# A four-layer graph network on one core: preparation that starts with the layer norm, and one visit per gathered block

## The chip, the cores and the metric

The kernel runs on one core of a Trainium2 chip. The metric is device time in microseconds (us). Engine names are those of the profile: PE is the matrix engine (PEld its weight loads), DVE the vector engine, ACT the scalar engine, POOL the engine that issues the indirect DMAs here, SP the engine that issues most plain DMAs. A name with a q behind it (SPq, POOLq) is that engine's instruction queue.

## What is computed

There are 6250 nodes with 256 features and 100000 edges (src, dst), the edges sorted by dst. The input is layer-normed and cut at zero, then four times each node adds the sum of its in-neighbours and goes through a three-matrix perceptron; the result is added to the input.

```python
def agg(h):
    return jax.ops.segment_sum(h[src], dst, num_segments=N)
for l in range(NL - 1):
    h = x + agg(x)
    h = jax.nn.relu(h @ W1s[l] + b1s[l])
    h = jax.nn.relu(h @ W2s[l] + b2s[l])
    x = h @ W3s[l] + b3s[l]
h = x + agg(x)
h = jax.nn.relu(h @ cW1 + cb1)      # cW1 256x256
h = jax.nn.relu(h @ cW2 + cb2)      # cW2 256x64
return h @ cW3 + cb3                # cW3 64x256
# around it: h = relu(layernorm(x)); x = x + network(h)
```

## The kernel before

The nodes are 49 blocks of 128. `XY` holds, in SBUF, all blocks of the current layer, already multiplied by that layer's W1 (the last W3 and the next W1 are multiplied together ahead, `fused`), as a high part and a rest so that two fast fp32r products give an fp32 one. The layers are called l0 to l3 here. Sums over neighbours are made in two ways.

*Products.* For about half of the blocks, a matrix of edge counts (uint8) is built once, in l0, out of one-hot rows of the edges (`build`: one-hots `lo` and `hi` on DVE at L1035, their product on PE at L1076, two copies per step to the matrix by ACT at L1084 and by DVE at L1086, in turn). It is kept in DRAM (`mats`), fetched again in each later layer in chunks of seven blocks (`fetch`), cast to fp32r (`prepare`, L1565) and multiplied with XY on PE: L1588 block by block in l0, L1665 by panels of four blocks after it (`product`). A unit of a panel is one block of XY: four matmuls with 512 columns. These matmuls are called `agg` below, by the tile that they write.

*Gathers.* For the other blocks (23 in l0, 20 in l1, 20 in l2, 19 in l3, 82 in all) the rows of the neighbours are fetched from the layer's table in DRAM: 17 tiles of 128 rows per block, each by one indirect DMA that POOL issues (L1382, 1394 in all, called rows below), and summed on PE by products with one-hots (`hot`, made by DVE at L1402) in a visit (`add`, L1419). `ROUNDS` gives two visits per block, of 11 and 12 matmuls over 8 and 9 tiles.

The order of the work is fixed while the program is written. `tick` counts units of the products, `passed` adds the estimated PE time of each product to a clock, and `Gathered.flow` issues a gather each time that clock has moved by a pace that spreads a layer's gathers over the layer. `meets` says when a visit is due: when the clock has reached the time of its last gather (the first one `LEAD` = 21 us after `begin`), or 8 units ahead of the layer's end. `begin(l+1)` comes when every block of the table of layer l+1 is written: after the perceptron of the last gathered block (block 48) and of the last panel. Those blocks' perceptrons are written out in three steps (transposes at L1479; L1225/L1233, L1245 and L1287/L1290) among the next layer's first products. In the page a line that carries PE `ps` is of these steps.

Ahead of the products stands the preparation. `look` finds, from the edge list, where each half block's edges start and what the lists of rows are: a first gather of the edges near each start (`near_i`), 17 counts over them (11 on DVE at L695, 6 on ACT at L698), an index chain, and then some 45 gathers of edge windows by POOL, called by `ask`. `normed` loads the input (`xs`), makes the statistics (`moments`, L879/L880), scales (L899), transposes, multiplies with W1 (L908, L920) and writes XY (L932 to L940), for 25 pairs of blocks. `fused` multiplies W3 and W1. All three are generators that the loop at the start of the kernel turns by `next`: it runs `look` and `fused` to the end of the index chain first, and then the 25 pairs with the rest of `look` between them.

Of the kernel before, what the change touches and what calls it, by code (L numbers as in the profile page):

```python
# [17 lines left out]
P = 128  # L18
# [378 lines left out]
def sorted_edges(  # L397
# [59 lines left out]
    ROUNDS = ((3, 1, -1), (0, 4, 2))  # L457
# [3 lines left out]
    NEAR = 11 * P  # L461
# [36 lines left out]
    rel = const.tile([P, left[NQ] // T, len(ROUNDS), 3, P // Q], BF16, name="rel")  # L498
# [58 lines left out]
    def fused(pool, w3_aps, w1_aps):  # L557
# [9 lines left out]
        load(1)  # L567
        yield
        for l in range(NLAYER):
            w3, w1 = loaded[l]  # L570
            w3t = pool.tile([P, KC, C], F32, name="w3t", bufs=1)
# [6 lines left out]
            b3b = pool.tile([P, KC, P], F32, name="b3b", bufs=1)  # L578
            nc.gpsimd.tensor_copy(b3b, b3[l][:, :, None].to_broadcast([P, KC, P]))
            yield  # L580
            w = pool.tile([P, KC + 1, C], F32, name="w31", bufs=1)
            for i in range(KC + 1):
                ps = ps_m.tile([P, W], F32, name="ps")
                for k in range(KC):
                    left = w3t[:, k, i * P:(i + 1) * P] if i < KC else b3b[:, k, :]
# [4 lines left out]
            load(l + 2)  # L590
# [26 lines left out]
    def look(pool):  # L617
        firsts_i = pool.tile([1, EB], I32, name="near_i", bufs=1)
        with nc.allow_non_contiguous_dma(reason="each tile's first destination"):
# [6 lines left out]
        nc.sync.dma_start(out=run[:FULL, :], in_=bass.AP(tensor=dst.tensor, offset=dst.offset,  # L626
                                                         ap=[[EC, FULL], [1, EC + 1]]))
        nc.sync.dma_start(out=run[FULL:FULL + 1, :E - FULL * EC],
                          in_=dst[FULL * EC:E].rearrange("(o e) -> o e", o=1))
# [15 lines left out]


        half = pool.tile([P, 2], F32, name="half", bufs=1)
        junk = pool.tile([P, NEAR], BF16, name="junk", bufs=1)
        for h in range(2):
# [3 lines left out]
                             start=True, stop=True)  # L653
            nc.vector.tensor_scalar(junk[:NSUB, e0:e1], ps[:NSUB, :e1 - e0], low[:NSUB, 0:1], None,
# [11 lines left out]
        )  # L666
        yield
# [24 lines left out]
        DV = 11  # L692
        for q in range(GSUB + 1):
            if q < DV:
                nc.vector.tensor_scalar(junk[:NSUB], near[:NSUB], float(GD * q), None,  # L695
                                        op0=OP.is_lt, op1=OP.add, accum_out=less[:NSUB, q:q + 1])
# [4 lines left out]
        nc.vector.tensor_scalar(less[:NSUB, DV:], less[:NSUB, DV:], -0.5, float(NEAR // 2),  # L701
                                op0=OP.mult, op1=OP.add)
        first = pool.tile([P, GSUB + 1], F32, name="first", bufs=1)
        nc.vector.tensor_scalar(first[:NSUB], less[:NSUB], at[:NSUB, 0:1], None, op0=OP.add)
        starts = pool.tile([NSUB, GSUB], I32, name="starts", bufs=1)
        nc.vector.tensor_scalar(starts, first[:NSUB, :GSUB], float(E - P), None, op0=OP.min)
        wd = pool.tile([P, GSUB, P], I32, name="wd", bufs=1)
        ws = pool.tile([P, GSUB, P], I32, name="ws", bufs=1)
        for q in range(GSUB):
            for w, e in ((wd, dst), (ws, src)):  # L710
                asks.append((w[:NSUB, q, :], e, starts[:, q:q + 1]))
        ask(4)
# [4 lines left out]
        sel = pool.tile([P, NQ, PW], F32, name="near_i", bufs=1)  # L717
# [17 lines left out]
        nc.vector.tensor_tensor(sel[:NSUB], sel[:NSUB], some[:NSUB], OP.mult)  # L735
        ps = ps_m.tile([P, W], F32, name="ps")
        for q in range(NQ):
            nc.tensor.matmul(ps[:PW, NV * q:NV * q + NV], sel[:NSUB, q, :], both[:NSUB, :],
                             start=True, stop=True)
        spread = pool.tile([P, NQ, NV], F32, name="spread", bufs=1)  # L740
# [77 lines left out]
        for w, (q0, q1) in ((3, (0, NQ - 1)), (4, (NQ - 1, NQ))):  # L818
            rows = gone[q0][1] * T
            nc.vector.tensor_reduce(wrong[:rows, w:w + 1], off[:rows, q0:q1, :],  # L820
                                    axis=mybir.AxisListType.XY, op=OP.max)
        ask(len(asks))
# [8 lines left out]
        yield  # L831
# [957 lines left out]
```

## Time and profile before

| | us |
|---|---|
| median of 3 runs | 2129.72 (2128.97 to 2136.23) |
| the profiled execution | 2135.8, its span 2134.0 |
| preparation: start to the last write of XY | 124.7 |
| first build steps, up to the first product | 124.7 to 142.7 |
| gathers of l0 / l1 / l2 / l3, issue of the first to the last | 126.6–674.2 / 719.2–1163.3 / 1205.7–1647.6 / 1686.8–2105.0 |
| last gather to the end of the span | 29.0 |

The profile puts 2057.4 us of the span on PE as busy time (96%), 1445.4 us on POOL (68%), 937.7 on DVE and 864.3 on ACT. The row of PE's waits has 15.0 us on gathered rows, in 12 waits. In the timeline rows of the trace, a row is a run of like instructions: start, busy time, engine, line, operation, tiles, count, and in brackets the idle time ahead of it with what ended it. A visit of 11 or 12 matmuls shows as 22 or 24 PE records, since an fp32 matmul leaves two. In the window rows, each engine's busy time stands with its count of instructions in brackets, then the clock that PE was granted, the DMA share and GB/s.

### The profile page before, as it was taken

To read this page: it belongs to the slowest core of one execution; us is meant where nothing else is said; L and a number is where in the kernel's file an instruction comes from. 1 tells how busy PE (TensorE), PEld (TensorE's weight loads), DVE (VectorE), ACT (ScalarE), POOL (GpSimd) and SP (SyncE) were. 2 spreads that over 40 slices of the span, in tenths; PEclk is the share of its full clock that TensorE was granted. 3 is DMA by queue.
4 is the path that set the end of the run, shared out by engine and by line. 5 is a ranking of instruction groups with operands and counts; after the bars stand their busy time and mean duration, and the time that the engine had idled before them with its cause. 6 is when DMAs were issued, how large, how long until landed. Compare 5 with 4: busy or idle time off the path is not lost.

```text
span 2134.0 us, 33393 instructions
## 1 busy us (share of the span) xinstructions
PE 2057.4 (96%) x12076; PEld 1487.8 (70%) x12076; DVE 937.7 (44%) x2192; ACT 864.3 (41%) x1775; POOL 1445.4 (68%) x1470
## 2 busy tenths in 40 slices
PE   4979999999999999999999999999999999999997
PEld 3756766667667777777776777777776777777675
DVE  7877867667673422222233322222233433333332
ACT  4856655556556522323232433222333432223231
POOL 2727777777774477777776377777776277777773
PEclk9979999999999999999999999999999999999999
DMA  5524545545455655455455554555456555556553
GB/s 157 176 98 139 162 142 153 158 140 164 150 158 152 213 163 155 153 181 164 142 186 167 173 160 148 173 165 169 146 168 195 170 172 181 184 180 194 183 160 119
DMA packets 184901, 347.61 MB, mean 163 GB/s; under 512 B 32446, under 2 KB 118496, under 8 KB 184726
## 3 DMA queue, kind: packets, MB, share of 16 engines
q0 software_dynamic: 68960, 185.41, 29.7%
q1 hardware_dynamic: 113838, 158.12, 22.3%
q8 instruction: 97, 1.59, 0.3%
q10 hardware_dynamic: 1928, 1.85, 0.3%
q14 instruction: 78, 0.64, 0.1%
HBM read 287.98 MB, written 57.26 MB: 162 GB/s over the span
## 4 chain that ended last, share of the span: by engine, by line
PE 88%; DVE 5%; DMA 4%; issue 1%; ACT 1%; POOL 1%; SPq 0%; DVEq 0%; POOLq 0%; ACTq 0%
PE agg L1665 43%; PE agg L1588 16%; PE sums L1419 11%; PE ps L1233 6%; PE ps L1290 6%; PE bp L1076 4%; DMA rows<-table,idx 3%; PE ps L1479 1%; POOL rows L1382 1%; DVE junk L695 1%; PE bp L920 1%; DVE hi L1035 1%; DVE at L1086 1%; PE ps L1245 0%; DMA table<-zs 0%
## 5 line engine op out<-in xcount | busy, mean ns | idle before, releaser
L1382 POOL DMA_INDIRECT rows<-table,idx x1394 | 1387.7, 995 | 611.4 <-issue 220.6
L1665 PE MATMUL agg<-a,XY 128*128 128x512 f32 x4116 | 982.8, 395 | 1.9 <-DVE clT L1600 1.9
L1665 PEld LDWEIGHTS agg<-a,XY 128*128 128x128 f32 x4116 | 764.6, 188 | 209.5 <-issue 45.8
L1565 ACT CAST a<-at 128x512 fp32r<-128x512 uint8 (+1 forms) x542 | 326.9, 616 | 576.9 <-PE agg L1665 543.9
L1565 DVE CAST a<-at 128x512 fp32r<-128x512 uint8 x543 | 242.7, 448 | 552.8 <-PE agg L1665 469.3
L1588 PE MATMUL agg<-XY,a 128*128 128x512 f32 x1470 | 404.9, 409 | 1.3 <-DVE un L1600 0.7
L1588 PEld LDWEIGHTS agg<-XY,a 128*128 128x128 f32 x1470 | 258.9, 189 | 53.7 <-issue 8.7
L1419 PE MATMUL sums<-rows,hot 128*32 128x256 f32 x3772 | 256.0, 385 | 16.2 <-DMA rows<-table,idx 15.0
L1419 PEld LDWEIGHTS sums<-rows,hot 128*32 128x32 f32 x3772 | 112.6, 109 | 142.6 <-issue 53.6
L1549 ACT CAST a<-at 128x512 fp32r<-128x512 uint8 (+2 forms) x362 | 196.7, 574 | 6.5 <-PE agg L1588 6.5
L1084 ACT CAST at<-bp 128x392 uint8<-128x392 f32 x240 | 116.6, 487 | 203.7 <-PE bp L1076 191.0
L1086 DVE CAST at<-bp 128x392 uint8<-128x392 f32 x240 | 135.1, 563 | 138.2 <-PE bp L1076 138.2
L1448 DVE TENSOR_TENSOR u<-u,sums 128x256 f32<-128x256 f32 x82 | 34.3, 419 | 241.8 <-PE agg L1665 226.9
L1076 PE MATMUL bp<-hi,lo 128*128 128x196 bf16 x960 | 127.5, 255 | 11.0 <-DVE hi L1035 10.7
L1290 PE MATMUL ps<-w,h 128*128 128x256 f32 x588 | 133.9, 379 | 1.4 <-ACT h L1236 0.9
L1233 PE MATMUL ps<-h,w 128*128 128x512 f32 (+3 forms) x332 | 133.9, 545 | 0.6 <-DVE zz L1298 0.6
L1035 DVE TENSOR_TENSOR hi<-cols,pairs 128x784 bf16<-128x784 bf16 x240 | 134.3, 560 | 0.0
L1076 PEld LDWEIGHTS <-lo 128*128 128x128 bf16 x960 | 70.6, 99 | 81.9 <-DVE hi L1035 27.8
L1290 PEld LDWEIGHTS ps<-w,h 128*128 128x128 f32 x588 | 111.1, 190 | 18.7 <-ACT h L1236 1.8
L1483 ACT ACTIVATE h<-ps,bias 128x256 f32<-128x256 f32 (+1 forms) x116 | 47.2, 464 | 154.9 <-PE ps L1479 154.9
L1298 DVE TENSOR_TENSOR zz<-ps,w 128x512 f32<-128x512 f32 (+1 forms) x75 | 50.1, 678 | 117.0 <-PE ps L1290 117.0
L1035 DVE TENSOR_TENSOR lo<-lanes,pairs 128x512 bf16<-128x512 bf16 x240 | 100.3, 418 | 1.3 <-ACT pairs L1030 1.3
(171 smaller groups left out, 989.7 us busy)
## 6 DMA issues: line engine op xcount, KB each, us to landing
at<-mat SPq DMA_DIRECT2D x151, 448.0 KB
mat<-at SPq DMA_DIRECT2D x30, 784.0 KB
rows<-table,idx POOLq DMA_INDIRECT x1394
table<-zz SPq DMA_DIRECT2D x72, 256.0 KB
back<-table SPq DMA_DIRECT2D x99, 128.0 KB
xs<-in_x_dram SPq DMA_DIRECT2D x8, 768.0 KB
table<-zs SPq DMA_DIRECT2D x24, 256.0 KB
out_dram<-zz SPq DMA_DIRECT2D x24, 256.0 KB
```

The costliest lines, as they stand in the source:

```text
L1035: nc.vector.tensor_tensor(o.rearrange("p q (n t) -> p q n t", t=2), values.rearrange("p (n t) -> p n t", t=2)[:, None, :, :].to_broadcast( ...
L1076: mm = nc.tensor.matmul(bp[:, m * HW:(m + 1) * HW], lo[:, q + m, :], hi[:, q + m, :], start=True, stop=True)
L1084: nc.scalar.copy(o, v)
L1086: nc.vector.tensor_copy(o, v)
L1233: mm = nc.tensor.matmul(ps[:mp, :w], weights[l][0][:, c, i * P:i * P + mp], h1[:, c, :w], start=(c == 0), stop=(c == KC - 1))
L1290: mm = nc.tensor.matmul(o, h2[0][:, c, nodes], w3[:, c, :], start=(c == 0), stop=(c == KC - 1))
L1382: got = nc.gpsimd.indirect_dma_start(out=t, out_offset=None, in_=tables[self.l][:, :], in_offset=bass.IndirectOffsetOnAxis(ap=idx[:, o:o + ...
L1419: nc.tensor.matmul(self.sums[m * Q:(m + 1) * Q, :C], self.hot[:, (c - min(rounds)) // 2, m, :], self.rows[g, c + 4 * m], start=(c == ROUND ...
L1549: nc.scalar.copy(a[:, i * m * P:(i + 1) * m * P].rearrange("p (j d) -> p j d", j=m), counts[b][:, j:j + m, :])
L1565: cast(o, at[:, :, d:d + m * P])
L1588: mm = nc.tensor.matmul(agg, a[:, d:d + P], XY[:, j, :], start=(j == 0), stop=(j == NT - 1))
L1665: mm = nc.tensor.matmul(agg[c][:, :w], XY[:, j, o:o + P], a[:, :w], start=(j == 0 and half == 0), stop=(j == NT - 1 and half == 1))
```

## The change

1. *Preparation.* The loop over the pairs starts at once, and `look` is turned by one stage at each of its steps (28 stages, 30 steps), `fused` by one in the first nine. The counts (`less`) are spread one or two to a step: 8 on DVE and 9 on ACT, over 1280 edges in place of 1408; the windows of four starts are asked for as soon as their counts stand (`settled`), three gathers per step in the first nine steps, then two. The moments of the first pair stand ahead of `look`'s second stage; the moments run 4 pairs ahead in place of 6. Stages end where DVE would need the result of PE (`yield` behind matmuls). The two loads of `run` stand behind the first two loads of xs; W3 and W1 of the second layer are loaded one stage later; the copy `b3b` on POOL is gone.
2. *Build.* The first 24 copies of the build are all on ACT.
3. *Visits.* `ROUNDS` has one visit per block, of 23 matmuls over 17 tiles. Its one-hots are made 4 units after the visit before; `hot` is one buffer of 768 columns in place of two of 384. The lead becomes `MARGIN` = 6 us and one visit's 17 gathers.
4. *The layers' ends.* In l1 and l2 the last visit may stand behind the layer's own products, up to 10 units into the next layer (`LATE`, `TAIL`; l0 and l3 keep the values of before). `open_one` keeps the old layer's visits first. Products take the seven chunks of XY in the order 0, 1, 3, 4, 5, 6, 2.
5. *Buffers.* 27 gather tiles in place of 25, 8 casts in place of 9 in l1 to l3.

DVE in the preparation, where the counts stand. Before (`junk,less` is a count, L891/L892 end a group of moments):

```order
L891 RECIPROCAL rstd<-std 128x6
L892 SCALAR_TENSOR_TENSOR shift<-mv,rstd 128x6
L689 TENSOR_SCALAR near<-near_i,low 98x1408
L695 TENSOR_SCALAR junk,less<-near 98x1408 x11
L701 TENSOR_SCALAR less<-less 98x6
L704 TENSOR_SCALAR first<-less,at_f 98x17
L706 TENSOR_SCALAR starts<-first 98x16
L720 TENSOR_SCALAR both<-first,since 98x1
```

The same place in the change, a few steps on:

```order
L904 RECIPROCAL rstd<-std 128x6
L905 SCALAR_TENSOR_TENSOR shift<-mv,rstd 128x6
L699 TENSOR_SCALAR less<-less 98x2
L701 TENSOR_SCALAR first<-less,at_f 98x4
L705 TENSOR_SCALAR starts<-first 98x4
L713 TENSOR_SCALAR junk,less<-near 98x1280
L945 COPY zs<-bp 128x512
L892 BN_STATS stats<-xs 128x6
L893 BN_AGGR mv<-stats 128x2
```

The eleven counts in a row are now single ones, with the pairs' moments and copies (`zs`) between them.

PE where l1 passes into l2. Before, the last visits of l1 (both halves of block 48's, `sums`) stand 32 `agg` matmuls ahead of the end of l1's products:

```order
L1665 MATMUL agg<-a,XY 128x512 x16
L1479 MATMUL ps<-ident,u 128x128 x2
L1479 MATMUL ps<-ident,clT 128x128 x2
L1419 MATMUL sums<-rows,hot 32x256 x23
L1665 MATMUL agg<-a,XY 128x512 x8
L1479 MATMUL ps<-ident,u 128x128 x2
L1665 MATMUL agg<-a,XY 128x512 x4
```

In the change the visit of block 48 stands 36 `agg` matmuls behind that end:

```order
L1700 MATMUL agg<-a,XY 128x512 x20
L1506 MATMUL ps<-ident,u 128x128 x2
L1506 MATMUL ps<-ident,clT 128x128 x2
L1700 MATMUL agg<-a,XY 128x512 x8
L1446 MATMUL sums<-rows,hot 32x256 x23
L1700 MATMUL agg<-a,XY 128x512 x8
L1506 MATMUL ps<-ident,u 128x128 x2
L1256 MATMUL ps<-h_12329,w_8629 128x512 x4
```

The visit, and behind it the perceptron of block 48 and so the start of l2's gathers, moved by 68 `agg` matmuls.

PE at the end of l3, from the last visit on. Before:

```order
L1419 MATMUL sums<-rows,hot 32x256 x12
L1665 MATMUL agg<-a,XY 128x512 x8
L1479 MATMUL ps<-ident,u 128x128 x2
L1665 MATMUL agg<-a,XY 128x512 x8
L1245 MATMUL ps<-clT,h_20696 128x256 x4
L1665 MATMUL agg<-a,XY 128x512 x12
L1233 MATMUL ps<-h_20730,w_16886 64x128 x2
L1665 MATMUL agg<-a,XY 128x512 x8
L1287 MATMUL ps<-clT,h_20786 128x256
```

In the change:

```order
L1446 MATMUL sums<-rows,hot 32x256 x23
L1700 MATMUL agg<-a,XY 128x512 x8
L1506 MATMUL ps<-ident,u 128x128 x2
L1700 MATMUL agg<-a,XY 128x512 x4
L1248 MATMUL ps<-h_20413,w_16837 64x256 x4
L1700 MATMUL agg<-a,XY 128x512 x12
L1268 MATMUL ps<-clT,h_20534 128x256 x4
L1700 MATMUL agg<-a,XY 128x512 x12
L1256 MATMUL ps<-h_20522,w_16837 64x128 x2
L1700 MATMUL agg<-a,XY 128x512 x8
L1310 MATMUL ps<-clT,h_20595 128x256
L1700 MATMUL agg<-a,XY 128x512 x20
```

Behind both stand the last panel's own two steps. 64 `agg` matmuls follow the last visit, where 36 did.

Counted over the whole order of PE from the first product on (a group is a run of matmuls of one kind, the build's left out; block 48's last step is what `begin` of the next layer stands behind):

| place on PE | groups, before | after | `agg` matmuls, before | after |
|---|---|---|---|---|
| last visit of l1 | 463 | 422 | 2663 | 2731 |
| last step ahead of `begin` of l2's gathers | 477 | 431 | 2723 | 2771 |
| last visit of l2 | 591 | 519 | 4080 | 4120 |
| last step ahead of `begin` of l3's gathers | 604 | 531 | 4136 | 4168 |
| last visit of l3 | 717 | 622 | 5550 | 5522 |
| the end | 732 | 640 | 5586 | 5586 |

The core of the diff:

```diff
-    ROUNDS = ((3, 1, -1), (0, 4, 2))
+    ROUNDS = ((3, 1, -1, 0, 4, 2),)
-    NEAR = 11 * P
+    NEAR = 10 * P
...
-        DV = 11
-        for q in range(GSUB + 1):
-            if q < DV:
-                nc.vector.tensor_scalar(junk[:NSUB], near[:NSUB], float(GD * q), None,
-                                        op0=OP.is_lt, op1=OP.add, accum_out=less[:NSUB, q:q + 1])
-            else:
-                nc.scalar.activation(junk2[:NSUB], near[:NSUB], AF.Sign, bias=edge[:NSUB, q:q + 1],
-                                     accum_out=less[:NSUB, q:q + 1])
-                yield
...
+        for q in range(0, GSUB, 2):
+            nc.vector.tensor_scalar(junk[:NSUB], near[:NSUB], float(GD * q), None,
+                                    op0=OP.is_lt, op1=OP.add, accum_out=less[:NSUB, q:q + 1])
+            for k in (q + 1,) if q + 2 < GSUB else (q + 1, q + 2):
+                nc.scalar.activation(junk2[:NSUB], near[:NSUB], AF.Sign, bias=edge[:NSUB, k:k + 1],
+                                     accum_out=less[:NSUB, k:k + 1])
+            yield
+            if q % 4 == 2:
+                settled(q - 2, q + 2)
+        settled(GSUB, GSUB + 1)
...
-        for t0 in range(0, 4 * G, G):
+        for t0 in (0, G):
             load(t0)
         yield
-        for s in range(G):
+        moments(0)
+        yield
+        for t0 in (2 * G, 3 * G):
+            load(t0)
+        for s in range(1, LEAD):
             moments(s)
...
+            next(looked)
+            next(rows)
             next(looked)
...
+            next(rows)
             next(looked)
-            next(rows)
-            turn_biases()
-            for _ in range(2 * NLAYER):
-                next(looked)
-                next(ahead_w)
-            next(looked)
-            STAGES = (*range(4, 20, 2), 20, 22, 24)
+            STAGES = (*range(16), 17, *range(17, 28))
             for i, _ in enumerate(rows):
-                ask(2)
+                ask(3 if i < 9 else 2)
+                if i == 1:
+                    turn_biases()
+                if i < 2 * NLAYER + 1:
+                    next(ahead_w, None)
                 if i in STAGES:
                     next(looked, None)
...
-                    if step % 2:
+                    if step % 2 or step <= 2 * PRE:
                         nc.scalar.copy(o, v)
...
-                return now[0] >= ends[self.l] - 8 or clock[0] >= self.first + (
+                return now[0] >= ends[self.l] + LATE[self.l] or clock[0] >= self.first + (
                     self.upto[self.done + 1] - self.upto[1]) * self.pace
             def begin(self):
-                self.first = clock[0] + LEAD
-                self.end = begun[self.l] + work_of(self.l) - TAIL
-                self.pace = (self.end - self.first) / (self.upto[-1] - self.upto[1])
+                self.one_hots(0)
+                self.end = begun[self.l] + work_of(self.l) - TAIL[self.l]
+                self.pace = (self.end - clock[0] - MARGIN) / self.upto[-1]
+                self.lead = MARGIN + self.upto[1] * self.pace
+                self.first = clock[0] + self.lead
...
                 if self.done < self.n:
-                    self.one_hots(self.done)
+                    later(4, lambda v=self.done: self.one_hots(v))
...
-        LEAD, TAIL = 21.0, 10.0
+        MARGIN = 6.0
+        TAIL = [10.0] + [-5.0] * (NLAYER - 1) + [10.0]
+        LATE = [-8] + [10] * (NLAYER - 1) + [-8]
...
-            for j in range(NT):
+            for at, j in enumerate(c * CH + i for c in CHUNKS for i in range(CH)):
...
-        rings = ctx.enter_context(tc.tile_pool(name="rings2", bufs=AHEAD + 6))
+        rings = ctx.enter_context(tc.tile_pool(name="rings2", bufs=AHEAD + 5))
-        gath = ctx.enter_context(tc.tile_pool(name="gath2", bufs=25))
+        gath = ctx.enter_context(tc.tile_pool(name="gath2", bufs=27))
```

More of the change, by code (lines that the diff above doesn't have):

```diff
@@ L971, in sorted_edges @@
             next(rows)
+            ahead_w = fused(prep, [W3s[l] for l in range(NLAYER)],
+                            [W1s[l + 1] for l in range(NLAYER - 1)] + [cW1])
+            next(ahead_w)
             make_identity(nc, ident)
@@ L1158, in sorted_edges, with split @@
         BACK = 3
-        def split(j, m, z):
+        fresh = set()
+        def split(l, j, m, z):
+            fresh.update((l + 1, k) for k in range(j, j + m))
             nc.scalar.copy(XY[:, j:j + m, :C], z[:, :m, :])
@@ L1661, in product @@
                 a = ring.pop(u)
+                assert (l, j) in fresh, (l, j, now[0], ends[l - 1], [k for k in range(NT) if (l, k) not in fresh], len(queue), layers[l - 1].done)
                 for c in range(KC):
```

114 lines of the change are left out of this document (66 added, 48 removed).

## The prediction

> **What bounds the kernel now.** I read the page first, for the engine that is busy throughout and for the one whose instructions never get shorter.
>
> ```profile
> span 2134.0 us, 33393 instructions
> PE 2057.4 (96%) x12076; PEld 1487.8 (70%) x12076; DVE 937.7 (44%) x2192; ACT 864.3 (41%) x1775; POOL 1445.4 (68%) x1470
> L1382 POOL DMA_INDIRECT rows<-table,idx x1394 | 1387.7, 995 | 611.4 <-issue 220.6
> ```
>
> PE looks like the bound at 96%. But POOL's gathers take 995 ns each, and 220.6 us more went by ahead of them in "issue", that is, in nothing that the profile shows. So a row costs POOL clearly more than its busy time, and 68% can be full. The windows by layer show where: from the first gather of a layer to the last one, and the gaps between.
>
> ```profile
> 719.00:1163.00 444.00, 442.57 (x2517) 324.02 (x2515) 132.61 (x305) 140.76 (x258) 336.67 (x339) 1.00 0.56 173
> 1163.00:1205.00 42.00, 37.64 (x155) 27.05 (x156) 13.34 (x31) 14.60 (x32) 0.99 (x2) 0.92 0.28 85
> 1205.00:1648.00 443.00, 443.00 (x2520) 325.00 (x2518) 132.31 (x297) 138.86 (x251) 333.72 (x340) 1.00 0.56 173
> 1648.00:1687.00 39.00, 35.69 (x163) 26.05 (x163) 14.79 (x34) 15.57 (x34) 0.78 (x2) 1.00 0.31 95
> 1687.00:2105.00 418.00, 411.98 (x2452) 303.16 (x2452) 135.31 (x299) 125.39 (x226) 319.88 (x322) 1.00 0.58 183
> 2105.00:2134.00 29.00, 18.41 (x98) 10.87 (x94) 8.22 (x19) 3.13 (x7) 0.95 (x1) 0.85 0.24 81
> ```
>
> Columns are PE, PEld, DVE, ACT, POOL. In l1 and l2 PE has work in practically every microsecond, and POOL issues 340 rows in 443 us, 1.30 each. In l3 POOL issues 322 in 418, also 1.30 each, while PE idles for 6 us. The same 1.30 with PE full and with PE waiting: I take it as POOL's own rate. So l1 and l2 end when PE is done, with POOL close behind, and l3 ends when POOL is done. The gaps of 42 and 39 us are those in which the next table is not complete.
>
> ```profile
> PE sums L1419 <- DMA rows<-table,idx: 15.0, 12, 3.3
> 1159.03 1.92 PE L1419 MATMUL sums<-rows,hot 128*32 128x256 f32 x26
> 1161.35 0.62 PE L1419 MATMUL sums<-rows,hot 128*32 128x256 f32 x2 [0.40 <-DMA rows<-table,idx]
> 1163.55 0.64 PE L1419 MATMUL sums<-rows,hot 128*32 128x256 f32 x8 [1.58 <-DMA rows<-table,idx]
> 1167.38 1.92 PE L1419 MATMUL sums<-rows,hot 128*32 128x256 f32 x10 [3.19 <-DMA rows<-table,idx]
> 1169.22 3.78 PE L1665 MATMUL agg<-a,XY 128*128 128x512 f32 x8
> 1172.81 0.56 PE L1479 MATMUL ps<-ident,u 128*128 128x128 f32 x2
> 1652.49 1.05 PE L1419 MATMUL sums<-rows,hot 128*32 128x256 f32 x10 [3.28 <-DMA rows<-table,idx]
> ```
>
> Of PE's 15.0 us of waits on rows, 5.2 (.40+1.58+3.19) stand at l1's last visits and 3.3 at l2's.
>
> **The price of a group on PE.** Every visit breaks a run of `agg` matmuls.
>
> ```profile
> 1127.18 1.50 PE L1419 MATMUL sums<-rows,hot 128*32 128x256 f32 x24
> 1128.61 3.94 PE L1665 MATMUL agg<-a,XY 128*128 128x512 f32 x16
> 1132.38 3.60 PE L1233 MATMUL ps<-h,w 128*128 128x512 f32 x8
> 2086.57 8.48 PE L1665 MATMUL agg<-a,XY 128*128 128x512 f32 x36
> 2094.89 0.60 PE L1479 MATMUL ps<-ident,u 128*128 128x128 f32 x4
> ```
>
> Start to start, 16 `agg` take 3.77 us and 36 take 8.32, so one is .2275 and .13 is left for the change of group. A visit of 12 is 1.43, so .108 each, and a visit of 23 is 2.49 + .13.
>
> **Up to l3's first gather.** By the table of counts, 73 groups fewer stand ahead of it (604 to 531): −9.5. But 32 more `agg` do (4136 to 4168), since block 48's step moved into the next layer: +7.3. Net −2.2. The 5.2 and 3.3 of waits have some 68 and 40 matmuls of cover more, 15 and 9 us, and go. With them goes the slow stretch behind the first: 1167.38 to 1169.22 is 1.84 for five matmuls worth .67, and the eight `agg` take 3.59 where 1.95 is right, 2.8 together. These three are −11.3. What is late next: l0's last visit wants 17 rows where its second half wanted 9 and is not moved, for which I put +2 (between 0 and the 3.3 of the longest wait). In l2 PE's own work from `begin` to the last visit is 1349 `agg` (307), 20 visits and 88 groups (59), and the perceptrons' matmuls, some 81 from their rows: 447, against 340 rows at 1.30 and 4 of landing, 446. That is level, where l1 keeps 18 us; +2 for it, between 0 and 5. So, counted from the first product, l3's first gather comes 2.2 + 11.3 − 2 − 2 = 9.5 earlier; the ends are 13.5 (neither of the two late ones) and 5.2 (3.3 and 5 of them).
>
> **l3 and the end.** The 323 gathers take 418 as before. PE's own work to the last visit sinks from some 409 to 390 (1354 `agg`, 19 visits, 91 groups, 26 of perceptrons), so POOL has more than 30 us of room to be waited for, and nothing that PE saves here counts. Behind the last visit there are 64 `agg` in place of 36, +6.4, and three more groups, +.4. So from the first product on: −9.5 + 6.8 = −2.7, with ends −6.7 and +1.6. POOL takes most of what PE gives.
>
> **Preparation.** Here the windows show DVE.
>
> ```profile
> 9.30:125.00 115.70, 88.85 (x416) 68.48 (x414) 96.40 (x270) 74.71 (x160) 54.99 (x64) 0.93 0.49 152
> 48.40:91.00 42.60, 40.60 (x211) 32.30 (x210) 40.86 (x117) 35.15 (x77) 33.27 (x33) 0.98 0.60 178
> 91.00:125.00 34.00, 28.91 (x132) 22.65 (x130) 23.25 (x67) 20.29 (x47) 12.88 (x11) 0.85 0.38 118
> 22.80 0.94 DVE L689 TENSOR_SCALAR near<-near_i,low 98x1408 f32<-98x1408 int32 x1
> 23.77 1.62 DVE L695 TENSOR_SCALAR_CACHE_REDUCE junk<-near 98x1408 bf16<-98x1408 f32 x1
> 25.44 1.62 DVE L695 TENSOR_SCALAR_CACHE_REDUCE junk<-near 98x1408 bf16<-98x1408 f32 x1
> 41.95 0.17 DVE L701 TENSOR_SCALAR less<-less 98x6 f32<-98x6 f32 x1
> 48.38 0.42 DVE L879 BATCH_NORM_STATS2 stats<-xs 128x6 f32<-128x256 f32 x1
> 123.72 1.02 DVE L940 TENSOR_TENSOR XY<-zs,XY 128x512 fp32r<-128x512 f32 x2
> ```
>
> DVE is 96% busy up to 91 and 68% after it, where the pairs wait in the chain through PE. The counts go from 11 at 1.67 (23.77 to 25.44) to 8 at 1.52 (10/11): −6.2 of DVE; ACT, at 74.7 of 115.7, takes three more. Two ways to the new end agree. By busy time: 96.4 − 6.2 = 90.2, at 96% 94.0, from 9.3 on: 103; and the 10.8 idle of 91 to 125, which is the drain of the chain: 114. By steps: the 30 steps from 48.38 to 124.7 took 2.5 each with `look`'s rest in them; the new ones carry also its chain (41.95 to 48.38, 6.4) and eight counts (12.2), +.62: 30 × 3.1 from 22 on is 116. I take 115, −10; ends are 103 (−21) and 124.7 (0). The gathers of windows start at four counts instead of all, and at POOL's rate they fill some 60 us, so they hide. `run`, the later loads and POOL's missing copy: nothing, as first readers come steps later; cover gone, a load waits under 2.
>
> **First build steps.**
>
> ```profile
> 126.89 0.42 DVE L1035 TENSOR_TENSOR lo<-lanes,pairs 128x512 bf16<-128x512 bf16 x1
> 127.23 0.56 DVE L1035 TENSOR_TENSOR hi<-cols,pairs 128x784 bf16<-128x784 bf16 x1
> 127.71 0.56 DVE L1086 CAST at<-bp 128x392 uint8<-128x392 f32 x1
> 128.18 0.42 DVE L1035 TENSOR_TENSOR lo<-lanes,pairs 128x512 bf16<-128x512 bf16 x1
> 125.00:142.00 17.00, 5.69 (x12) 0.61 0.45 151
> 131.70 0.83 PE L1076 MATMUL bp<-hi,lo 128*128 128x196 bf16 x4 [0.45 <-DVE hi L1035]
> ```
>
> DVE does a double step in 1.29 (126.89 to 128.18), .47 of it the copy; PE waits for DVE. Twelve copies go to ACT, which then has two of .47 (5.69 for 12, the window row of L1084) per double step, .95. So ACT sets the step: 12 × (1.29 − .95) = −4; ends −5.7 (DVE alone) and 0.
>
> **Sum.** −10 − 4 − 2.7 = −16.7, on the execution's 2135.8: 2119. The median lies 6.1 lower, at 2129.72: 2113. All the good ends give −21 − 5.7 − 6.7 = −33, 2096; the bad ones 0 + 0 + 1.6, 2131. Hot's single buffer, the casts' ring and the chunk order: nothing, DVE is at 44% and the visits' one-hots stand 4 units, some 4 us, after the last use; the two more gather tiles are POOL's and I see no idle of POOL for want of one.
>
> **The clock.** After 5.2 us of waits PE worked at half rate from 1167.38 on, 2.8 us lost (above). In l3 the change makes 32 us of waits in 19 visits, 1.7 each, some of them twice that. The Trainium skill ("TensorE: Matmul & The Clock Gate", Part 1) says that one idle window of about 3.4 us sets the half rate; the trace agrees, with the .92 of clock in the window 1163 to 1205 beside 1.00 in the window that follows. By that rule single waits of 1.7 would do nothing and the sum stays; where waits come in a row between late rows, it is the last rival below.
>
> **Rivals.**
> - *The pairs don't come earlier.* For: `look`'s stages stand in each step, and ACT, with 9 counts, the scales and the W copies, sits in the pairs' chain. Against: DVE's 96%, so it had been DVE. Then −6.7: 2123.
> - *Slower: a step of the preparation waits.* A stage of `look` that needs POOL or PE holds DVE, and now the pairs with it. At 4.5 per step the preparation ends at 22 + 135 = 157: +32 − 6.7, 2155. It decides from 4.0 per step on (142: +17.3 − 6.7, which is .5%). For: nine steps have a count each on DVE (1.52) and ACT, a W stage on PE and three gathers, 3.9 us at 1.30; against: 2.5 per step so far, while ACT and PE had room.
> - *PE is the bound throughout.* All 92 groups (−12), all 15.0 of waits, the slow stretch (−2.8) and −14 of the start: 2086. It needs l3's gathers at 390/323, 1.21 each; no layer shows that.
> - *Half clock in l3.* If half of the 19 waits set it off at 2.8 each, those intervals are 23.3 in place of 22: 9.5 × 1.3 = +12, 2125. It limits itself, as a slowed PE no longer waits.
>
> **How the numbers follow.** My forecast 0.49, the pairs no earlier 0.23, slower 0.16, PE the bound 0.06, half clock 0.06. About 0.5%, 10.6 us, is what a measurement tells from no change, so the bounds are 2119 and 2140. Faster: most of the forecast (.43), PE the bound (.06), and a part of the first rival (.05): 0.54. Slower: 0.16. Same: the rest, 0.30. The range 2098 to 2138 leaves out PE the bound and the slower case past 2138, some 0.2.
>
> **What would show it.** The last write of XY near 115; the double build steps near .95, bound by ACT's copies; no row wait at l1's and l2's ends, but several in l3, one per visit; rows in l3 at 1.30 without a gap; from the last gather to the end some 35 in place of 29. It is wrong if steps of the preparation take 3.5 or more, or if l2's last visit waits long, as POOL's 446 there has no room.

## The result, and the profile after

| | before | after |
|---|---|---|
| median, us (20 runs each) | 2132.12 (2127.09 to 2138.86) | 2127.77 (2123.40 to 2133.76) |
| ratio, with its 95% interval | | 0.9978 (0.9970 to 0.9987) |
| the profiled execution, us | 2135.8 | 2128.08 |

The change gains 4.4 us, .2%, where 16.7 were forecast. The page of the profile after, its first rows and the costliest groups that answer to those shown of before:

```profile
span 2126.3 us, 33236 instructions
PE 2034.3 (96%) x12076; PEld 1495.9 (70%) x12076; DVE 925.0 (44%) x2103; ACT 872.8 (41%) x1793; POOL 1445.9 (68%) x1467
L1407 POOL DMA_INDIRECT rows<-table,idx x1394 | 1388.8, 996 | 595.7 <-issue 225.7
```

The windows from a layer's first gather to its last one, and the gaps, as in the prediction (PE, PEld, DVE, ACT, POOL, clock, DMA share, GB/s):

```profile
714.00:1168.00 454.00, 453.59 (x2569) 341.03 (x2568) 143.04 (x306) 149.23 (x272) 337.83 (x340) 1.00 0.57 175
1168.00:1195.00 27.00, 27.00 (x154) 20.16 (x153) 10.44 (x26) 12.70 (x29) 0.87 (x2) 1.00 0.38 117
1195.00:1636.00 441.00, 437.78 (x2497) 327.68 (x2495) 130.63 (x277) 140.16 (x252) 336.50 (x340) 1.00 0.56 173
1636.00:1668.00 32.00, 30.27 (x164) 22.64 (x163) 12.56 (x28) 12.57 (x29) 0.56 (x1) 1.00 0.32 99
1668.00:2092.00 424.00, 397.66 (x2358) 293.86 (x2356) 129.13 (x267) 120.78 (x214) 319.20 (x323) 0.98 0.57 176
2092.00:2126.30 34.30, 26.73 (x164) 17.57 (x162) 10.79 (x24) 5.50 (x11) 0.68 (x1) 0.95 0.31 94
PE sums L1446 <- DMA rows<-table,idx: 33.3, 15, 6.2
```

PE no longer waits at l1's end (27.00 of 27 us busy), and the next layer's gathers start 27 and 33 us after the last ones, where it was 42 and 39. In l3 it waits: 26 us of 424 idle, at a clock of .98 instead of 1.00. The stages side by side, forecast beside measured (the third column of times is a second profile of the change, below as c1):

| stage, us | before | after | after, again | forecast of the change | measured |
|---|---|---|---|---|---|
| start to the end of the last write of XY | 124.7 | 118.8 | 119.0 | −10 | −5.9, −5.7 |
| from there to the first product | 18.0 | 15.8 | 15.7 | −4 | −2.2, −2.3 |
| first product to l3's first gather | 1544.1 | 1533.8 | 1534.7 | −9.5 | −10.3, −9.4 |
| l3's first gather to its last | 418.2 | 423.3 | 419.8 | 0 | +5.1, +1.6 |
| last gather to the end | 29.0 | 34.6 | 35.1 | +6.8 | +5.6, +6.1 |
| span | 2134.0 | 2126.3 | 2124.3 | −16.7 | −7.7, −9.7 |

The span of before lies 7.7 and 9.7 us above the two of the change, while the medians differ by 4.4. Of this, 3.4 us come from the choice of executions: the profiled one of before lies 3.7 above its median of 20 runs, that of the change .3 above its own. Which stage of before holds these 3.7 isn't known, so a difference in the table can be too large by as much.

The preparation, by windows, and DVE's rows at its waits and at its end:

```profile
9.30:48.40 39.10, 29.41 (x116) 21.47 (x117) 27.58 (x86) 24.48 (x51) 12.09 (x23) 1.00 0.58 179
48.40:91.00 42.60, 33.20 (x180) 24.87 (x179) 38.81 (x116) 33.62 (x71) 28.97 (x28) 1.00 0.61 181
91.00:118.80 27.80, 23.49 (x125) 18.60 (x123) 25.20 (x73) 19.68 (x46) 13.22 (x11) 1.00 0.32 100
...
26.00:36.00 10.00, 10.00 (x44) 8.42 (x43) 6.23 (x20) 7.17 (x15) 0.99 (x1) 1.00 0.47 149
36.00:46.00 10.00, 8.52 (x43) 6.76 (x42) 6.93 (x19) 9.16 (x20) 6.78 (x7) 1.00 0.41 124
...
30.89 0.17 DVE L699 TENSOR_SCALAR less<-less 98x2 f32<-98x2 f32 x1 [3.53 <-ACT near_i L716]
39.90 0.69 DVE L953 TENSOR_TENSOR XY<-zs,XY 128x512 fp32r<-128x512 f32 x1 [2.83 <-ACT XY L949]
117.80 1.02 DVE L953 TENSOR_TENSOR XY<-zs,XY 128x512 fp32r<-128x512 f32 x2
120.03 0.96 DVE L1430 TENSOR_TENSOR hot<-colf,rel 128x768 f32<-128x768 f32 x1 [1.21 <-DMA table<-zs]
120.90 0.42 DVE L1053 TENSOR_TENSOR lo<-lanes,pairs 128x512 bf16<-128x512 bf16 x1
```

DVE's busy time from 9.3 on is 91.6 us (27.58 + 38.81 + 25.20), near the forecast (90.2). But 11.5 us of the first 39 it stands idle. Before, it stood idle for 6.8 of the same 39:

```profile
9.30:48.40 39.10, 19.34 (x76) 13.53 (x75) 32.28 (x89) 19.27 (x39) 8.84 (x22) 0.94 0.48 153
```

Of the 11.5, the two waits on ACT's results shown above make 6.4, and two waits for loads (`xs` and `near_i`), both before 21.2, make 3.9. PE is busy for all of 26 to 36 (the W products beside the first pairs), and ACT for 9.16 of the next 10 us: it has a count of 1.55, the scales and the W copies in each step. From 48 to the end DVE is busy to 91%, and what was idle at the end before (10.8 us from 91 on) is down to 2.6.

The first build steps on ACT, from its first copy to the cast for the first product, before and then in the change:

```profile
127.40 0.48 ACT L1084 CAST at<-bp 128x392 uint8<-128x392 f32 x1 [1.21 <-PE bp L1076]
142.03 2.18 ACT L1549 CAST a<-at 128x512 fp32r<-128x512 uint8 x4
...
122.37 3.52 ACT L1102 CAST at<-bp 128x392 uint8<-128x392 f32 x8 [2.07 <-PE bp L1094]
133.95 2.19 ACT L1582 CAST a<-at 128x512 fp32r<-128x512 uint8 x4
```

That is 14.6 us before and 11.6 in the change.

What l3's waits look like, on PE and on POOL:

```profile
1865.17 0.63 PE L1446 MATMUL sums<-rows,hot 128*32 128x256 f32 x6
1871.99 5.16 PE L1446 MATMUL sums<-rows,hot 128*32 128x256 f32 x40 [6.19 <-DMA rows<-table,idx]
1877.09 6.68 PE L1700 MATMUL agg<-a,XY 128*128 128x512 f32 x28
...
1874.06 0.96 POOL L1407 DMA_INDIRECT rows<-table,idx  x1 [0.30 <-issue]
1878.10 0.95 POOL L1407 DMA_INDIRECT rows<-table,idx  x1 [3.09 <-PE agg L1700]
```

Three matmuls run (two records each), and the fourth, which reads tile 15 of 0 to 16, waits for it. The 20 from there on take 5.1 us, where .108 each makes 2.2: the clock granted from 1870.1 to 1876.8 is .50. POOL's next gather stands behind a matmul that is behind the visit, so it loses 2.8 us (3.09 less the usual .3). Within l3, POOL has three such gaps above 1 us (1.49, 3.09 and 2.58) in this profile and two (1.09 and 2.46) in the second one, that is 6.3 and 3.0 us beyond the usual .3; before has none.

### The profile page after: what moved, and what is told of

It reads as the page before. It is cut to its first block, busy times and chain, and to the rows that moved or that the text cites. A ratio compares the mean times of both kernels' runs of the same rounds, so it can differ in the third digit from the quotient of the medians.

```text
span 2126.3 us, 33236 instructions
## 1 busy us (share of the span) xinstructions
PE 2034.3 (96%) x12076; PEld 1495.9 (70%) x12076; DVE 925.0 (44%) x2103; ACT 872.8 (41%) x1793; POOL 1445.9 (68%) x1467
## 4 chain that ended last, share of the span: by engine, by line
PE 86%; DMA 4%; DVE 3%; issue 1%; ACT 1%; POOL 1%; DVEq 0%; SPq 0%; POOLq 0%; ACTq 0%
PE agg L1700 43%; PE agg L1622 15%; PE sums L1446 11%; PE ps L1256 6%; PE ps L1313 6%; PE bp L1094 4%; DMA rows<-table,idx 4%; PE ps L1506 1%; DVE hi L1053 1%; POOL rows L1407 1%; DVE at L1104 1%; PE ps L1268 1%; PE ps L1248 0%; DVE lo L1053 0%; ACT at L1102 0%
## 5 line engine op out<-in xcount | busy, mean ns | idle before, releaser
L1446 PE MATMUL sums<-rows,hot 128*32 128x256 f32 x3772 | 248.3, 391 | 33.5 <-DMA rows<-table,idx 33.3
L1446 PEld LDWEIGHTS sums<-rows,hot 128*32 128x32 f32 x3772 | 124.0, 111 | 151.0 <-DMA rows<-table,idx 46.1
L1102 ACT CAST at<-bp 128x392 uint8<-128x392 f32 x252 | 121.5, 490 | 186.9 <-PE bp L1094 181.3
L1104 DVE CAST at<-bp 128x392 uint8<-128x392 f32 x228 | 128.6, 564 | 137.4 <-PE bp L1094 135.0
```

The costliest lines, as they stand in the source:

```text
L1102: nc.scalar.copy(o, v)
L1104: nc.vector.tensor_copy(o, v)
L1446: nc.tensor.matmul(self.sums[m * Q:(m + 1) * Q, :C], self.hot[:, c - min(rounds), m, :], self.rows[g, c + 4 * m], start=(c == ROUNDS[0][0] ...
```

## The experiments

The runs fell on two kinds of chips. On one (here A) before takes 2130.6 us, near the first result; on the others (B) 2363 to 2392, with the same program: PE's waits have rows "issue" there (waits for nothing that the profile shows) that A doesn't have. Ratios are to before on the same chip. The change itself on A:

> The changed kernel itself, as the yardstick of the three runs beside it on this chip. Both theories: 0.998 of before on a chip like that of the first result. On the chip of the four runs before, where the gathers took 1.5 us each in all layers and PE waited in issue beside its visits, there is no yardstick; this one tells whether a run beside it can be compared with the first result (before near 2132 us) or only with this one.

Measured on A: 2125.77, ratio 0.9979 (0.9964 to 0.9994): the yardstick of the next three.

### Do the gathers set l3?

```diff
+                self.full = 16 if l == NLAYER else T
                 self.order = [(g, k) for g, rounds in self.visits for k in self.tiles(rounds)
+                              if k < self.full]
...
-                                self.hot[:, c - min(rounds), m, :], self.rows[g, c + 4 * m],
+                                self.hot[:, c - min(rounds), m, :], self.rows[g, min(c + 4 * m, self.full - 1)],
```

> The changed kernel, but in l3 each visit fetches 16 tiles in place of 17; the matmul of the missing tile uses the 16th once more, so one tile of each block's rows is left out of the sums of l3 and another counted twice. PE's work is unchanged. Theory (the gathers set l3's time): 19 gathers fewer at 1.30 us, -25 us, until PE's own 390 us set it; so 20 to 28 us faster than the change, near 0.987 of before. Rival (PE sets the time, its waits are a by-product): the waits on rows shrink, the end moves by 0 to -5, 0.996 of before.

> As for the first run of this kernel (16 of 17 tiles gathered per visit in l3, the same PE work): theory (the gathers set l3's time) 20 to 28 us faster than the change; rival (PE sets it) 0 to 5 faster. On a chip where PE is short of issue, that is where before takes some 2390 us, also the theory expects less, some 5 to 10, since the gathers are no longer what l3 waits for.

On A: 2103.16, 0.9867 (0.9851 to 0.9884), 22.6 us faster than the change with the same matmuls. The windows of l3, of this run and then of the change beside it:

```profile
1668.00:2066.00 398.00, 390.46 (x2356) 292.18 (x2355) 128.45 (x267) 120.71 (x214) 300.52 (x303) 1.00 0.58 181
```

```profile
1669.00:2089.00 420.00, 397.95 (x2353) 293.24 (x2352) 127.42 (x265) 120.53 (x214) 318.63 (x322) 0.98 0.57 178
```

PE's busy time even sinks by 7.5, and the clock is back at 1.00: l3 goes by its gathers, 1.31 each, and at 398 us they are now close to the 390 of PE's own busy time. On B: 2369.61, 0.9899 (0.9875 to 0.9922), more than expected there; the gathers of l3 took 451 us, where the change took 477 and its other variants on B 480 to 490. A gather costs 1.49 there in the mean, but the median one is as on A, .96 with a gap of .30: in l3 of the change on B, 47 of 321 gathers have longer gaps, 61 us together beyond .30, and a matmul ends some two thirds of that. So what 1.49 has above A's 1.30 is for the most part waiting for PE, and no price of POOL's own. Why 19 gathers fewer gain more there isn't settled.

### Do PE and POOL hold each other up?

```diff
-        MARGIN = 6.0
+        MARGIN = [6.0] * NLAYER + [11.0]
...
```

> The changed kernel with MARGIN 11 in place of 6 in l3 alone, so that some four more gathers stand ahead of each visit in the order. Theory (PE and POOL wait for each other: a gather written behind a visit is tied to a matmul behind it, and the visit waits for its own rows): POOL's waits on PE in l3 fall from 72 us of idle time (112 times) to before's 38 (124 times), the gathers of l3 take 418 us in place of 423, the end comes 5 us earlier, near 0.9955 of before. Rival (the 5 us are the gathers' own, from the DMA side): 423 stays, 0.998.

> MARGIN 11 in l3. Theory (PE and POOL wait for each other): the gathers of l3 take 418 us in place of 423, 5 us faster than the change. Rival (the 5 us are the gathers' own): no difference.

On A: 2125.79, 0.9971 (0.9959 to 0.9982), that is, no faster than the change, where 5 us were expected. But in the profiles l3's gathers did come faster, 414.8 us in place of 419.8; from the last one to the end it took 37.6 in place of 35.1. PE's rows at the last two visits show what ate half of it:

```profile
2061.33 0.63 PE L1446 MATMUL sums<-rows,hot 128*32 128x256 f32 x6
2067.87 4.97 PE L1446 MATMUL sums<-rows,hot 128*32 128x256 f32 x40 [5.91 <-DMA rows<-table,idx]
...
2090.03 2.80 PE L1446 MATMUL sums<-rows,hot 128*32 128x256 f32 x46
```

The wait of 5.9 us left PE at half clock, so that it came to the last visit late and found all rows there. On POOL's side the sum of waits on PE hardly fell (71.9 and 68.8 us in the two profiles of the change, 64.4 here, for an expected 38), as most of it is the usual .3 per gather; what went is the gaps above 1 us, of which there is none left in l3. So the theory holds for the gathers. For the time it fell: 2.4 of the 4.9 us came back as PE's, and of the rest the medians show nothing (this profile lies 1.7 below its median). On B: 2400.66, 1.0030 (1.0014 to 1.0047).

### What stands behind the last visit

```diff
-        TAIL = [10.0] + [-5.0] * (NLAYER - 1) + [10.0]
-        LATE = [-8] + [10] * (NLAYER - 1) + [-8]
+        TAIL = [10.0] + [-5.0] * (NLAYER - 1) + [2.0]
+        LATE = [-8] + [10] * (NLAYER - 1) + [-4]
```

> The changed kernel with TAIL of l3 at 2 in place of 10 and LATE at -4 in place of -8, so that 32 agg matmuls in place of 64 stand behind the last visit; nothing of PE's work changes. Theory (the last visit's time is set by the gathers, what stands behind it is added): 32 x 0.2275 = 7.3 us earlier, 27 us from the last gather to the end in place of 34.6, near 0.9945 of before. Rival (PE's work sets the end): no change, 0.998.

> 32 agg matmuls in place of 64 behind the last visit. Theory (the gathers set the last visit's time): 7 us faster than the change, 27 us from the last gather to the end. Rival (PE's work sets the end): no difference. On a chip where PE is short of issue: no difference by both.

On A: 2120.21, 0.9950 (0.9936 to 0.9964), 5.6 us faster than the change; the last gather is issued at 2087.4, the span ends 28.9 later (35.1). From the end of the last visit PE takes 15.7 us in place of 22.5. So its order at the end is worth what was counted, 32 matmuls (7.3 us), less .4 in which the last perceptrons, now closer together, wait longer for ACT and DVE. It is the fastest version on A that computes everything. On B: 2392.24, 0.9996 (0.9977 to 1.0016).

### The preparation undone, and alone

The first kernel is the change with `look`, `fused`, `normed` and the loop over them as they were before, the second is the kernel before with those of the change and the condition `step <= 2 * PRE` in the build.

> The changed kernel with the preparation of before (look, fused, normed and the loop that turns them; 11 and 6 counts over 1408 edges). Theory: all that the preparation gains, 6 us up to the last write of XY, goes through to the end, as every later stage starts from the first product: 6 us slower than the change, near 1.0005 of before. Rival (the preparation's gain is lost later, since the gathers of l1 to l3 are the bound): no slower than the change, 0.998.

> The changed kernel with the preparation of before. Theory (what the preparation gains goes through to the end): the last write of XY 6 us later than the change's 118.5, the end 6 us later than the change, 1.0007 of before. Rival (lost again in the gathers' phases): as the change, 0.998.

> The kernel before with the new preparation and the first 24 build copies on ACT, and the visits, ends and buffers of before. Theory: from the first product on, the change's two sides cancel (l3's gathers start some 10 us earlier and give it back in l3 and behind the last visit), so this alone has all that the change has: the first product 8 us earlier, 0.9965 of before and no slower than the change, within 3 us. Rival (the visits carry a gain of their own): 3 us or more slower than the change, 0.9995.

> The kernel before with the new preparation and the first 24 build copies on ACT, and the visits, ends and buffers of before; on a chip where before takes some 2132 us. Theory (from the first product on, the change's visits and ends gain and lose alike): first product at 134.7, the end 6 to 8 us earlier than before, no slower than the change, 0.9965 of before. Rival (the visits carry a gain of their own): 3 us or more slower than the change, 0.9995.

> The kernel before with the new preparation and build copies alone. On a chip where before takes some 2131 us: theory (the visits and ends gain nothing by themselves) 0.9965 and no slower than the change beside it; rival 0.9995, 3 us or more slower than the change. On a chip where before takes some 2390 us: 0.995 to 0.997 as before, faster than the change.

> The changed kernel once more, as the yardstick for the runs on chips where before takes some 2390 us (PE short of issue), if this call falls on one. Theory there: 1.003 of before, since the runs of the change with one thing altered lay at 1.003 to 1.005 and those with the later last visit at 1.000; so the visits and ends, without the preparation, cost some .7% there. Rival: 0.998 as on the other chip. On a chip where before takes some 2131 us: 0.998.

All fell on B, on four chips. There the change is slower than before, if only by .4%: 2373.49, 1.0037 (1.0019 to 1.0055). With the old preparation it is 1.0075 (1.0055 to 1.0096) and 1.0090 (1.0059 to 1.0122), and the preparation with the copies alone is 0.9950 (0.9932 to 0.9967), 0.9972 (0.9958 to 0.9985) and 0.9945 (0.9924 to 0.9966). The old preparation ends its last write of XY at 131 to 137 there, in place of the 124.7 of the first profile, the new one at 118.7 to 120. So on B the preparation (with the copies, where it is alone) gains .3 to .55%, and the visits and layer ends cost .65 to .9%. The change and the preparation alone were timed on the same chip once, 2373.49 and 2352.01; that is .9%. PE's waits there, of before (on B) and then of the change:

```profile
PE agg L1665 <- issue: 54.4, 116, 1.6
PE sums L1419 <- issue: 10.0, 20, 1.5
```

```profile
PE sums L1446 <- issue: 71.5, 132, 1.7
PE agg L1700 <- issue: 10.2, 24, 2.1
...
1039.93 1.12 PE L1446 MATMUL sums<-rows,hot 128*32 128x256 f32 x16
1041.40 1.11 PE L1446 MATMUL sums<-rows,hot 128*32 128x256 f32 x3 [0.35 <-issue]
1042.81 2.27 PE L1446 MATMUL sums<-rows,hot 128*32 128x256 f32 x27 [0.30 <-issue]
```

With two visits these waits stand mostly behind them, in the `agg` matmuls; with one of double length they stand inside it. The visit shown takes 5.1 us to the next start in place of 2.73; those without a wait for rows take 4.9 in the mean on B and 2.75 on A. On A the preparation alone wasn't measured, as all three runs are from B; the table of stages stands in for it: from the first product to the end it was 1991.3 before, and 1991.7 and 1989.6 in the two profiles of the change. So on A, too, the visits and the layers' ends show no gain of their own, as far as a before profile that is 3.7 long can tell.

One more profile of before fell on B too (2394.94), so it doesn't show which stage made the 2135.8 on A long; this stays open:

> The kernel before, for one more profile. If the execution that the sum was made against was a long one, as its 2135.8 beside medians of 2130.6 and 2132.1 says, then this profile shows in which stage: theory, in l3 and behind it (gathers of l3 under 418 us or less than 29 behind them), as the stages up to l3 have no waits that could vary; rival, spread over the layers.

### Counts from ACT to DVE

```diff
...
+            if q % 4 == 0:
+                nc.vector.tensor_scalar(junk[:NSUB], near[:NSUB], float(GD * (q + 1)), None,
+                                        op0=OP.is_lt, op1=OP.add, accum_out=less[:NSUB, q + 1:q + 2])
-            for k in (q + 1,) if q + 2 < GSUB else (q + 1, q + 2):
+            for k in () if q % 4 == 0 else (q + 1,) if q + 2 < GSUB else (q + 1, q + 2):
```

> The changed kernel with 12 counts on DVE and 5 on ACT in place of 8 and 9. Theory (from 36 to 56 us the steps of the preparation go by ACT, busy 9.1 of 10 us there, while DVE has 7 to 8): 4 x 1.57 us off ACT, the last write of XY 2 to 4 us earlier, near 115.5, 0.997 of before. Rival (DVE's sum sets the preparation): 4 x 1.53 more on DVE, 3 to 6 us later, 1.000.

On B: 1.0047 (1.0024 to 1.0070), beside 1.0037 for the change. The new preparation runs alike on both kinds of chips, so the trace can be read. Its windows from 36 to 56:

```profile
36.00:46.00 10.00, 9.14 (x47) 7.61 (x46) 8.57 (x23) 8.00 (x18) 6.69 (x8) 1.00 0.44 138
46.00:56.00 10.00, 8.26 (x40) 6.07 (x39) 9.69 (x26) 6.81 (x15) 6.90 (x7) 1.00 0.80 226
```

ACT is relieved and DVE fills up (9.69 of 10), but the last write of XY starts at 120.0, where the other runs with the new preparation have 118.3 to 119.6. Neither side had it. The first five steps, from the first write of XY to the sixth, took 24.6 us in place of 23.9, and all that follows the same 54.6. So four counts less on ACT gained nothing, and four more on DVE cost .7 of their 6.1 us. As the same run took work from one engine and gave it to the other in the same steps, it doesn't show which of them sets those steps; that stays open.

### The order inside a visit

Two orders were tried: the 23 matmuls by tile, and the six rounds of four as -1, 0, 1, 2, 3, 4. The first sorts the matmuls by tile where they are issued; the second is

```diff
-    ROUNDS = ((3, 1, -1, 0, 4, 2),)
+    ROUNDS = ((-1, 0, 1, 2, 3, 4),)
...
-                                start=(c == ROUNDS[0][0]), stop=(c == ROUNDS[-1][-1]))
+                                start=(c == (-1 if m else 0)), stop=(c == ROUNDS[-1][-1]))
```

> The changed kernel with a visit's 23 matmuls in the order in which their tiles are gathered (0 to 16); before, the fourth matmul already wants tile 15 of 0 to 16, so that 20 matmuls stand behind the wait for the second-last tile. Theory (a visit's wait in one lump, followed by half clock, is what makes l3 longer than its gathers): waits of over 3 us become pieces of 1.3, PE's clock in l3 rises from 0.98 to 1.00, the last visit ends 2 us earlier behind its last tile; the end 3 to 6 us earlier, 0.996 of before. Rival (only the gathers' rate counts): the end at most 2 earlier, that of the last visit, 0.997.

> The changed kernel with the six rounds of a visit in the order -1, 0, 1, 2, 3, 4 in place of 3, 1, -1, 0, 4, 2, four matmuls at a time beside each other as before; so the rounds want up to tile 11, 12, 13, 14, 15, 16 in turn, where the first one wanted tile 15. Theory (a visit's wait in one lump, with half clock behind it, makes l3 longer than its gathers): the waits of l3 come in pieces of 1.3, the 20 matmuls behind them become 4, the end 2 to 5 us earlier than the change, 0.9965. Rival (only the gathers' rate counts): at most 2 earlier, 0.997 to 0.998.

> Both: the rounds in order, and 32 agg matmuls behind l3's last visit. Theory: the gains add, 5.6 of the later last visit and 2 to 5 of the order, 0.993 of before. Rival (the order gains nothing): 0.995, as the later last visit alone.

All on B. By tile: 2514.46, 1.0515 (1.0478 to 1.0551). It can't answer its question, since it changed something else:

```profile
1020.23 6.32 PE L1445 MATMUL sums<-rows,hot 128*32 128x256 f32 x46
```

The 23 matmuls take 6.25 us to the next start, and no visit of this run takes less; at least a quarter of the change's visits on B take 2.73, as on A. Four neighbours of a round write four different quarters of the partitions; in the order of tiles most neighbours write the same quarter. The Trainium skill ("TensorEngine Tiling (Array Packing)", Tiling Modes and Key Properties) says that a 128x32 tiling has four tiles that work independently; the trace agrees, with a price that more than doubles where neighbours mostly use the same one. The rounds in order keep four: 2399.03, 1.0037 (1.0022 to 1.0051), no different from the change on B, where PE waits only 8.7 us for rows in all, so there was little to gain. With the later last visit: 2388.92, 0.9998 (0.9980 to 1.0017), that one's gain alone. Whether the order gains on A, where l3's lumps are, wasn't tried.

## Why the prediction was wrong in size

The forecast had the sign, and e1 and e3 bear out its main mechanism, that l3 goes by its gathers and that what stands behind the last of them is added. Of the five terms of its sum, two came as forecast and three fell short. Two of these, of the preparation and the first build steps, stayed within the ends given for them; the third, l3's gathers, had been put at no change, with no ends. The execution that the sum was made against did the rest.

- *"In l3 ... nothing that PE saves here counts"*: right. 19 gathers fewer, 24.7 us of POOL, move the end by 22.6 (e1).
- *"Up to l3's first gather", −9.5*: right as a sum, −10.3 and −9.4, but in part by luck. The waits at l1's end went as counted. But l0's last visit, at 668.0, takes 7.4 us in place of 2.7 (a wait of 2.38 and half clock behind it), 4.7 where 2 had been put, and l2's waits for rows make 4.9 and 3.4 where 2 had been put. So some 4 to 6 us came earlier than counted, which no run here separates.
- *"Behind the last visit there are 64 agg", +6.8*: right, +5.6 and +6.1, and 5.6 came back when 32 of them were moved ahead of it (e3).
- *"The 323 gathers take 418 as before"*: a failed step, +5.1 and +1.6 where 0 stood. The rate was right, and that POOL never waits for PE was not. PE's waits for rows in l3 make 26.0 and 21.7 us, in 11 and 12 waits (32 in 19 had been counted). They come in lumps of up to 6.2, as the visit's fourth matmul wants tile 15; PE goes on at half clock, and POOL's next gather stands behind a matmul behind the visit. POOL's gaps above 1 us cost 6.3 and 3.0 in the two profiles, and where they were gone the gathers took 414.8 (e2). That was the chain of the last rival, at 1.6 to 5.1 us where it had 12. Half clock alone is not the measure of it: both profiles have 17.1 us of it in l3. From the first product on the sum is +.4 and −1.7, for a forecast of −2.7.
- *"I take 115, −10"*: the step that failed most plainly, 118.8 and 119.0. DVE's sum was nearly right (91.6 beside 90.2); its share of time in the first 40 us was not. "DVE is 96% busy up to 91" holds from 48 on; from 9.3 to 48.4 it was 83% already before (32.28 of 39.10), and in the change it is 71%. I carried the 96% of a window in which DVE was the bound to a stretch in which it waits for loads and for ACT. The step count of 3.1 us has the same fault: five steps there (writes of XY at 39.9 and 63.8) took 4.8 each. That is above the 4.0 from which the rival "slower" was to hold, had it gone on for all 30 steps. What sets these first steps, PE, ACT or the order between them, stays open (e6).
- *"So ACT sets the step", −4*: ACT's copies set it, .97 us for each of the 12 double steps (11.6 in all), as forecast; yet −2.2. I left out that `begin` now makes the first visit's one-hots, .96 on DVE ahead of the first build: the first `lo` starts 2.08 behind the last write of XY, where it was 1.34, so .7 is lost. And the same copies took 14.6 us before, not the 12 × 1.29 = 15.5 of the sum, so .9 less could be saved.
- *"The median lies 6.1 lower"*: I took the sum from one execution to a median of three runs, as if before and after lay alike about their medians. Over 20 runs the profile of before lay 3.7 above, that of the change .3: 3.4 of the 12 us missing.

The rival in which the preparation gains nothing is refuted by 118.8, and on B by e5; that of PE as the bound throughout by e1. Forecast and result differ by 12.3: 4.1 preparation, 1.8 first build, 5.1 l3, 3.4 the execution, less some 2 of the two other terms. By the forecast's own prices PE's work in l2 and l3 would have been 449 and 393 us, not 447 and 390; no term of the sum hangs on that.

On the clock, the Trainium skill ("TensorE: Matmul & The Clock Gate", Part 1) has half rate after an idle window of some 3.4 us. These traces don't go by the length of one wait; the first row is of the change, the second of its second profile:

```profile
1736.96 4.42 PE L1446 MATMUL sums<-rows,hot 128*32 128x256 f32 x40 [2.38 <-DMA rows<-table,idx]
2071.86 1.93 PE L1446 MATMUL sums<-rows,hot 128*32 128x256 f32 x30 [3.47 <-DMA rows<-table,idx]
```

After a wait of 2.38 us 20 matmuls take 4.42, half rate; after one of 3.47, 15 take 1.93, the full one. In the trace of before, too, the longest wait ahead of the slow stretch was 3.19. What decides it isn't shown here.

## What to carry over

Where a second engine's fixed rate sets a stage, work saved on the busiest engine counts only up to that stage's start, and what is put behind the stage's last transfer counts in full; both can be counted from the order. An engine's share of a window may be used for a new schedule only where the same engine will be the bound: the 96% of 48 to 91 said nothing of the stretch ahead of it, which had 83% and then 71%. A transfer that is tied to a matmul behind a wait takes part in that wait, so the time that it takes where nobody waits is the least that it will take. A gain of .5% that comes as a sum of one profiled execution needs that execution's place among the other runs before it is set against a median.

## What the chips showed that I had not expected

The same program takes 2131 us on one chip and 2363 to 2392 on four others, at nearly the same clock (.99 and .96 to .98); the change is .2% faster on the first kind and .4% slower on the second (0.9979 and 1.0037). In the change's profile there PE has 113 us of waits "issue", 71.5 of them inside the long visits, which on A have none, and POOL's gathers come at 1.48 to 1.58 us each in place of 1.30 to 1.41. What PE waits for there isn't shown by any run here.
